# Multi-query attention on one core: in even steps a norm's small operation, a query product and the lower scores' addition change places with the upper reciprocals

## The chip, the cores and the metric

The kernel runs on 1 core of one Trainium2 chip. The metric is the device time of one execution in microseconds (us); less is better. A core has five engines, each with a queue of its own that it works off in order: TensorE (PE, with its weight loads shown as PEld), VectorE (DVE), ScalarE (ACT), GpSimd (POOL) and SyncE (SP), which here only issues DMAs.

## The reference

There are 64 sequences of 128 tokens with 512 features, all float32. The attention has 16 query heads of width 64 and one shared key and value head:

```python
xn = layernorm(x, g_in)
q = (xn @ Wq) * 64 ** -0.5            # 16 heads of 64
k, v = split(xn @ Wkv)                # one head of 64, and a null key and value in front
sim = q @ k.T + attn_bias             # causal, and masked by a mask per sequence
out = softmax(sim) @ v                # 16 heads of 64 -> 1024
out = layernorm(out @ Wo, g_out)
return x + out
```

## The kernel before, in words

A block is one sequence. Four blocks form a group, since the query projection of a group is worked out together. `step(n)` is called for n = -6 to 62; it holds, in an order written out by hand, pieces of work on many blocks: it multiplies attention weights and values of block n (`values`, `values_end`), takes the softmax of block eb = n + 1 and the scores of block nb = n + 2, projects a quarter of a later group's queries and finishes the output of earlier blocks. Every call puts its instructions at once at the end of the queues of the engines, so the order of calls in `step` is the order on each engine. Semaphore waits between engines are put in by the framework where a tile is read, written or used again. A pool's tile waits until all readers of the tile that had its buffer are done.

What the change and the prediction's steps touch:

- **Scores.** `scores(nb, hf)` is made of 32 small matmuls on PE into the one PSUM tile `ps` (lines L500); hf 0 is the lower half of the rows, whose causal keys are 64 of 128, hf 1 the upper half. `scores_add(nb, hf)` (DVE, L513) adds them to the bias and mask that POOL put in S (`bias_add`, L479). As there is one `ps` buffer, `scores(nb, 1)` waits for `scores_add(nb, 0)`. `scores_max` (DVE, L518) gives the maxima.
- **Softmax.** `exps(eb, hf, lo, hi)` is one exponential with a sum for each of the 8 rows of heads (ACT, L527). `rinv(eb, hf)` is the reciprocal of the sums (DVE, L544), `scale` multiplies by it (POOL, L548). `blocks_T` then transposes both halves together (DVE, L580) and `blocks_move` issues the DMAs (SP, L606) that put the pieces in `aTb` for `values` of the next step (PE, L641). `values` of split steps has a small DVE copy named `done` (L673).
- **Queries.** `product(qg, f, k, ...)` is one of seven products of a Strassen-like scheme (4 matmuls of 128x256, PE, L436); they go into the PSUM tiles a and c (one buffer each) and w (two buffers, shared with other tiles). `keep` copies one aside (ACT, L447), `q_out` writes a piece of the queries from PSUM (ACT, L454) or as a sum with a kept piece (DVE, L457). Product 3 of step n + 1 adds into tile c, after `q_out(qg, HC + f, hi_t, "c", "u3")` at the end of step n has read it.
- **Output.** Blocks p and p + 1 (p odd) are projected as a pair in seven products too (`out_product`, 8 matmuls, PE, L755; `out_keep`, L769 on ACT; `out_part`, L776 on ACT or L778 on DVE). `pair_stats` (DVE, L784 to L788), `pair_pow` (POOL, L792), `pair_nmr` (DVE, L799: one operation on 128x1), `pair_norm` (ACT, L809, `yn`) and `pair_residual` (DVE, L813 and L814) make norm and residual; p4 and p4 + 1 are the pair that is finished in a step.
- **Input norm.** `norm_stats` (DVE, L256 to L260; POOL, L261) and `norm_apply` (DVE, L273, `nmr`; ACT, L274) for block m, whose x was loaded by SP in an earlier step. SP also carries the loads of residuals (`res`), the tokens (`xd`, `xT`) and the stores.

In the even steps from 4 to 56, `first` and `third` hold (a pair's first products begin, another pair is finished), and `second` does not. The kernel before gives there, among others, this order:

```python
        if soft and n != 1:
            exps(eb, 1, 2, 4)
        if soft and not second:
            exps(eb, 1, 4, 6)
        if fast:
            product(qg, f, 1, ps_q, "a")
            keep("a", "p1")
            q_out(qg, f, lo_t, "w", "p1")
        if soft and not second:
            exps(eb, 1, 6)
            rinv(eb, 1)
            scale(eb, 1)
```

Of the kernel before, what the change touches and what calls it, by code (L numbers as in the profile page):

```python
# [17 lines left out]
def kernel(  # L18
# [87 lines left out]
    ps_q = ctx.enter_context(tc.tile_pool(name="ps_q", bufs=1, space=PSUM))  # L106
# [147 lines left out]
    def norm_stats(m):  # L254
        st = small.tile([P, 6], FP, tag="st", name=f"st_{m}")
        nc.vector.bn_stats(st, xs[m])  # L256
        mv = small.tile([P, 2], FP, tag="mv", name=f"mv_{m}")
        nc.vector.bn_aggr(mv, st)
        rstd = small.tile([P, 1], FP, tag="rstd", name=f"rstd_{m}")
        nc.vector.tensor_scalar(rstd, mv[:, 1:2], EPS, None, ALU.add)  # L260
        nc.gpsimd.tensor_tensor(rstd, rstd, nhalf, ALU.pow)  # L261
        stats[m] = mv, rstd
# [157 lines left out]
    def product(g, f, k, pool, tag, start=True):  # L420

        if start:
            prod[tag] = pool.tile([P, HT], FP, tag=tag, name=f"p{tag}_{g}_{f}_{k}")
        lo, hi = xT[g][:, 0 : GB // 2], xT[g][:, GB // 2 :]
        t1, t2, t3, t4 = (xS.get((g, i)) for i in range(1, 5))
        w, t = {
            1: (a11, lo[:, :, lo_k]),
            2: (a12, lo[:, :, hi_k]),
            3: (s4, hi[:, :, hi_k]),
            4: (a22, t4),  # L430
            5: (s1, t1),
            6: (s2, t2),
            7: (s3, t3),
        }[k]
        for kc in range(HK):
            nc.tensor.matmul(  # L436
                prod[tag],
                w[:, kc, f * P : (f + 1) * P],
                t[:, :, kc, :],
                start=(start and kc == 0),  # L440
                stop=(kc == HK - 1),
                skip_group_check=not start,
            )

    def keep(tag, name):
        kept[name] = bp.tile([P, HT], FP, tag=f"k{name}", name=f"k{name}", bufs=1)
        nc.scalar.copy(kept[name], prod[tag])  # L447

    def q_out(g, c, toks, tag, name=None):
        lo = toks.start // N  # L450
        o = q_part(g, c, lo, lo + 2)
        p = prod[tag].rearrange("p (t h i) -> p t h i", t=2, h=2)
        if name is None:
            nc.scalar.copy(o, p)  # L454
        else:
            k = kept.pop(name).rearrange("p (t h i) -> p t h i", t=2, h=2)
            nc.vector.tensor_tensor(o, p, k, ALU.add)  # L457
# [57 lines left out]
    def scores_max(b, hf):  # L515
        if hf == 0:
            nmax[b] = small.tile([P, 2, R8], FP, tag="nmax", name=f"nmax_{b}")
        nc.vector.tensor_reduce(  # L518
            nmax[b][:, hf], S[b][:, :, WITH_NULL[hf]], AX.X, ALU.max, negate=True
        )  # L520

    def exps(b, hf, lo=0, hi=R8):
        if hf == 0 and lo == 0:
            rsum[b] = small.tile([P, 2, R8], FP, tag="rsum", name=f"rsum_{b}")
        for k in range(lo, hi):
            row = S[b][:, k, WITH_NULL[hf]]
            nc.scalar.activation(  # L527
                row,
                row,
                AF.Exp,  # L530
                bias=nmax[b][:, hf, k : k + 1],
                accum_out=rsum[b][:, hf, k : k + 1],
            )
# [8 lines left out]
    def rinv(b, hf):  # L542
        rinvs[b, hf] = small.tile([P, R8], FP, tag="rinv", name=f"rinv_{b}_{hf}")
        nc.vector.reciprocal(rinvs[b, hf], rsum[b][:, hf])  # L544
# [178 lines left out]
    def plain(b):  # L723
        return not (paired(b) or paired(b - 1))
# [39 lines left out]
    def out_keep(tag, name, slot):  # L764
        kept[name] = bp.tile([P, HE], FP, tag=f"k{slot}", name=f"k{name}", bufs=1)
        if name == "yu2":
            nc.vector.tensor_copy(kept[name], prod["y" + tag])  # L767
        else:
            nc.scalar.copy(kept[name], prod["y" + tag])  # L769

    def out_part(b, e, tag, name=None):
        if b not in ys:
            ys[b] = hp.tile([P, DIM], FP, tag="y", name=f"y_{b}", bufs=3)
        o = ys[b][:, lo_e if e == 0 else hi_e]
        if name is None:
            nc.scalar.copy(o, prod["y" + tag])  # L776
        else:
            nc.vector.tensor_tensor(o, prod["y" + tag], kept.pop(name), ALU.add)  # L778
# [17 lines left out]
    def pair_nmr(b):  # L796
        mv, rstd = yn.pop(b)
        nmr = small.tile([P, 1], FP, tag="nmro", name=f"nmro_{b}")
        nc.vector.tensor_scalar(nmr, mv[:, 0:1], rstd, -1.0, ALU.mult, ALU.mult)  # L799
        nmrs[b] = nmr, rstd  # L800
# [61 lines left out]
    def step(n):  # L862
        def ok(b, end=B):
            return 0 <= b < end
# [11 lines left out]
        p12, p4, p5673 = n - 1, n - 3, n - 2  # L876
        first, third, second = paired(p12), paired(p4), paired(p5673)
        one = ok(n - 1) and plain(n - 1)
        def transfers():

            if n == 1:
                store(0)
            if n > B3 + 1 and ok(n - 2) and plain(n - 2):
                store(n - 2)
            loads_late(n)
# [22 lines left out]
                token_sum(qg, k)  # L908
        for m in mns:
            norm_stats(m)  # L910
        if n == -4:
            bias_add(0)
            bias_add(1)
# [42 lines left out]
        if n == B3 - 1:  # L956
            scores(B3 + 1, 1)
            scores_add(B3 + 1, 1)
            scores_max(B3 + 1, 1)
        if third:  # L960
            pair_stats(p4 + 1)
        if 2 * GB <= mb < B:
            tokens_T(mb)
            if (mb + 1) % GB == 0:
                tokens_out(mb // GB)
        if soft and n != 1:
            exps(eb, 0, 4)
        if fast and f == 0 and not fill:
            token_sum(qg, 1)
        if soft and n not in (1, B3 + 1):  # L970
            rinv(eb, 0)
            scale(eb, 0)
        if third:
            pair_pow(p4 + 1)
# [29 lines left out]
        if n == B3:  # L1004
            out_keep("X", "yp1", "p1")
            scores(eb, 0)
            scores_add(eb, 0)
            scores_max(eb, 0)
            out_product(p12, 2, ps_w, "w")
            pair_norm(p4)  # L1010
            pair_residual(p4)
            store(p4)
            out_part(p12, 0, "w", "yp1")
            scores(eb, 1)
            scores_add(eb, 1)
            exps_half(eb, 0)
            scores_max(eb, 1)
        elif first:
            out_keep("X", "yp1", "p1")
            out_product(p12, 2, ps_w, "w")  # L1020
            out_part(p12, 0, "w", "yp1")
        if soft and n != 1:
            exps(eb, 1, 2, 4)
        if soft and not second:
            exps(eb, 1, 4, 6)
        if fast:
            product(qg, f, 1, ps_q, "a")
            keep("a", "p1")
            q_out(qg, f, lo_t, "w", "p1")
# [20 lines left out]
        if fast and f == 0 and not fill:  # L1050
            for k in range(3, 5):
                token_sum(qg, k)
        if fast:
            product(qg, f, 5, ps_q, "c")
        if second:
            out_product(p5673, 7, ps_y, "X", start=False)
# [9 lines left out]
        if n == B3 - 1:  # L1066
            exps_half(B3 + 1, 0)
            exps(B3 + 1, 1, 0, 3)
        if sc and n != B3:
            scores(nb, 0)  # L1070
            scores_add(nb, 0)
        split = sc and n != B3
# [207 lines left out]
```

## Time and profile before

| | us |
|---|---|
| median of three runs | 1109.07 |
| the three runs | 1108.53, 1110.0, 1109.07 |
| the profiled execution | 1106.42 |
| its span, first to last instruction | 1104.5 |

| engine | busy us | share of the span |
|---|---|---|
| PE (matmuls) | 1081.3 | 98% |
| PEld (weight loads, beside the matmuls) | 868.1 | 79% |
| DVE | 795.7 | 72% |
| POOL | 706.0 | 64% |
| ACT | 665.5 | 60% |

The profile is of one execution. A row of a timeline has the start in us from the span's begin, the duration in us, engine, line, operation, the tiles out<-in, their shapes, and the count of instructions that were merged; in brackets stand the engine's idle time before it and what ended it. A row of the waits has the waiting engine and tile, what was waited for, the sum in us, the count and the longest. Busy times of different engines overlap; the idle time of an engine that is not the bound costs nothing.

### The profile page before, as it was taken

The page shows a single profiled execution, that of the slowest core. Times are in us where ns is not written, and L with a number is a line of the kernel's source. Part 1 is how long each engine was busy: PE and PEld are TensorE (multiplying, and loading weights), DVE is VectorE, ACT ScalarE, POOL GpSimd, SP SyncE. Part 2 cuts the span into 40 slices and gives each one's busy share as a digit, 9 for nine tenths or more (in the row PEclk, how much of TensorE's full clock was granted, in tenths as well). Part 3 has the DMA queues.
Part 4 walks back from the last instruction along what each step waited for, and adds up shares of the span by engine and source line. Part 5 has one row for each costly group of instructions (what it writes and reads, how often), then busy time and mean ns, then how long its engine had stood idle before and what let it go on. Part 6 is the DMA issues. An engine that isn't in the chain of part 4 may idle for free.

```text
span 1104.5 us, 27326 instructions
## 1 busy us (share of the span) xinstructions
PE 1081.3 (98%) x9794; PEld 868.1 (79%) x9794; DVE 795.7 (72%) x1729; ACT 665.5 (60%) x2645; POOL 706.0 (64%) x521
## 2 busy tenths in 40 slices
PE   8999999999999999999999999999999999999987
PEld 5576788888888888888888888888888888888643
DVE  4676677877867877776886777787777787666852
ACT  3265567666666656566756566766666665657651
POOL 2546958566676756767575675856667675676832
PEclk9999999999999999999999999999999999999999
DMA  6422354453534444353353435445353453422333
GB/s 198 129 76 62 81 150 112 134 131 89 159 99 139 125 128 122 91 167 107 121 138 113 126 101 149 115 131 132 87 159 99 134 130 116 113 63 76 97 106 100
DMA packets 101062, 129.81 MB, mean 118 GB/s; under 512 B 21312, under 2 KB 65728, under 8 KB 99136
## 3 DMA queue, kind: packets, MB, share of 16 engines
q1 hardware_dynamic: 99680, 126.70, 41.0%
q8 instruction: 78, 1.28, 0.5%
q10 hardware_dynamic: 1248, 1.38, 0.4%
q14 instruction: 56, 0.46, 0.1%
HBM read 54.86 MB, written 31.46 MB: 78 GB/s over the span
## 4 chain that ended last, share of the span: by engine, by line
PE 81%; DVE 5%; DMA 4%; ACT 4%; SPq 3%; POOL 2%; issue 1%; DVEq 0%; POOLq 0%; ACTq 0%
PE pa L436 17%; PE pyX L755 16%; PE pc L436 8%; PE pyY L755 8%; PE ps L500 8%; PE po L641 7%; PE pk L321 4%; PE pw L436 4%; PE pyw L755 4%; DMA x<-in_x_dram 3%; PE py L702 3%; ACT s L527 2%; SPq L606 2%; PE pq L387 1%; DVE s L513 1%
## 5 line engine op out<-in xcount | busy, mean ns | idle before, releaser
L527 ACT ACTIVATE s<-s,nmax 128x65 f32<-128x65 f32 (+1 forms) x1024 | 371.5, 367 | 0.0
L479 POOL TENSOR_TENSOR s<-biasp,mneg 128x1552 f32<-128x1552 f32 x64 | 205.3, 3208 | 112.0 <-DVE sb L580 108.8
L548 POOL TENSOR_TENSOR s<-s,rinv 128x512 f32<-128x512 f32 (+1 forms) x128 | 189.6, 1482 | 122.6 <-DVE nmro L799 89.1
L685 ACT ACTIVATE oT<-po,nv 128x512 f32<-128x512 f32 x128 | 81.0, 683 | 198.0 <-PE po L641 198.0
L527 ACT ACTIVATION_READ_ACCUMULATOR s<-s,nmax 128x1 f32 x1024 | 194.7, 190 | 0.0
L755 PE MATMUL pyX<-wT,oT 128*128 128x256 f32 x696 | 164.7, 379 | 0.5 <-DVE kyu L767 0.5
L755 PEld LDWEIGHTS pyX<-wT,oT 128*128 128x128 f32 x696 | 131.8, 190 | 19.6 <-DVE kyu L767 0.9
L500 PEld LDWEIGHTS ps<-kT,qT 64*64 64x64 f32 x4096 | 92.5, 134 | 48.1 <-DVE s L513 25.6
L513 DVE TENSOR_TENSOR s<-ps,s 128x512 f32<-128x512 f32 (+1 forms) x128 | 121.6, 950 | 10.1 <-PE ps L500 9.6
L436 PE MATMUL pa<-xS,wq 128*128 128x256 f32 x480 | 123.6, 380 | 1.0 <-ACT ku L447 1.0
L518 DVE TENSOR_REDUCE nmax<-s 128x8 f32<-128x520 f32 (+1 forms) x128 | 120.1, 938 | 1.3
L500 PE MATMUL ps<-kT,qT 64*64 64x64 f32 (+1 forms) x4096 | 116.7, 251 | 3.7 <-DVE done L673 2.0
L580 DVE STREAM_TRANSPOSE sb<-s 128x1536 f32<-128x1536 f32 x62 | 109.9, 1773 | 11.6 <-POOL s L548 4.3
L641 PE MATMUL po<-aTb,vs 64*64 64x256 f32 (+1 forms) x1240 | 115.3, 379 | 0.0
L436 PEld LDWEIGHTS pa<-xS,wq 128*128 128x128 f32 x480 | 86.2, 190 | 11.2 <-ACT ku L447 1.8
L447 ACT COPY ku<-pa 128x256 f32<-128x256 f32 x120 | 44.7, 373 | 82.5 <-PE pa L436 82.5
L261 POOL TENSOR_TENSOR rstd<-rstd,nhalf 128x1 f32<-128x1 f32 x64 | 35.7, 558 | 60.4 <-DVE rstd L260 55.4
L436 PE MATMUL pa<-xS,wS 128*128 128x256 f32 x240 | 67.8, 405 | 0.1
L809 ACT ACTIVATE yn<-y,nmro,rstdo 128x512 f32<-128x512 f32 x58 | 45.4, 782 | 36.2 <-DVE nmro L799 36.1
L321 PE MATMUL pk<-wkv,xT 128*128 128x128 f32 x488 | 64.5, 275 | 0.0
L457 DVE TENSOR_TENSOR qT<-pw,kp 128x256 f32<-128x256 f32 x60 | 25.4, 424 | 53.4 <-ACT kp L447 53.4
L641 PEld LDWEIGHTS po<-aTb,vs 64*64 64x64 f32 (+1 forms) x1240 | 55.8, 134 | 9.7 <-issue 4.1
(116 smaller groups left out, 2068.9 us busy)
## 6 DMA issues: line engine op xcount, KB each, us to landing
aTb<-sb SPq DMA_DIRECT2D x369, 64.0 KB
x<-in_x_dram SPq DMA_DIRECT2D x64, 256.0 KB
res<-in_x_dram SPq DMA_DIRECT2D x64, 256.0 KB
out_dram<-y SPq DMA_DIRECT2D x64, 256.0 KB
aTb<-sb SPq DMA_DIRECT2D x492, 32.0 KB
xd<-xb SPq DMA_DIRECT2D x14, 1024.0 KB
xT<-xd SPq DMA_DIRECT2D x56, 256.0 KB
wo<-in_L_cond_Wo_dram SPq DMA_DIRECT2D x1, 2048.0 KB
```

The costliest lines, as they stand in the source:

```text
L321: nc.tensor.matmul(pkv, xT[g][:, t, kc, :], wkv[:, kc, :], start=(kc == 0), stop=(kc == KC - 1),)
L436: nc.tensor.matmul(prod[tag], w[:, kc, f * P : (f + 1) * P], t[:, :, kc, :], start=(start and kc == 0), stop=(kc == HK - 1), skip_group_ch ...
L479: nc.gpsimd.tensor_tensor(S[b], biasp, mneg[:, t].unsqueeze(1).broadcast_to([P, R8, ROW]), ALU.add,)
L500: nc.tensor.matmul(pv[u * DH : (u + 1) * DH, r, f, :], qT[g][rows, f, t, hf, u], kT[b][rows, 0:nk], start=True, stop=True,)
L513: nc.vector.tensor_tensor(sv, pss.pop((b, hf)), sv, ALU.add)
L518: nc.vector.tensor_reduce(nmax[b][:, hf], S[b][:, :, WITH_NULL[hf]], AX.X, ALU.max, negate=True)
L527: nc.scalar.activation(row, row, AF.Exp, bias=nmax[b][:, hf, k : k + 1], accum_out=rsum[b][:, hf, k : k + 1],)
L548: nc.gpsimd.tensor_tensor(sv, sv, rinvs.pop((b, hf)).unsqueeze(2).broadcast_to([P, R8, sv.shape[2]]), ALU.mult,)
L580: nc.vector.transpose(sb.rearrange("p j e q -> p e j q"), S[b][:, :, 1 : ROW - 1].rearrange("p e (j k) -> p e j k", k=Q),)
L641: nc.tensor.matmul(pos[b][u][r * DH : (r + 1) * DH, half], vals[keys], aT_of(b)[keys, slots, r * NF : (r + 1) * NF], start=start, stop=Tru ...
L685: nc.scalar.activation(oT[b][:, u * NF : (u + 1) * NF, :].rearrange("p f (s q) -> p s f q", q=Q), po[u].rearrange("p h i f q -> p (h i) f q"),
L755: nc.tensor.matmul(prod[key], h[:, c, :], w[:, c, :], start=(start and c == 0), stop=(c == HC - 1), skip_group_check=not start,)
```

## The change

In the even steps that start one pair, finish another and project queries (`even`; n = 4, 6, ... 56, 27 steps), calls move:

- `pair_nmr(p4)` comes forward to just behind the input norm's statistics.
- The exponentials of the lower half, rows 4 to 8, keep their place on ACT; the lower reciprocal comes ahead of `pair_stats(p4 + 1)` and the token transpose on DVE.
- Query product 1, its copy and its `q_out` come ahead of the out product 2 and its `out_part`; the exponentials between them are dealt out anew around these copies.
- Product 5, the lower scores and their addition come ahead of the last two exponentials, the upper reciprocal, `pair_norm(p4 + 1)` and `norm_apply`. On PE product 5 and the lower scores keep their places; on DVE the addition now stands in front of the upper reciprocal, the `nmro` of block p4 + 1 and the `nmr` of the input norm.
- The kept piece `yp1` uses the slot u3 in place of p1, since p1 is now in use at the same time.

The order on POOL and on SP stays as it was.

```diff
+        even = first and third and fast
+
...
         for m in mns:
             norm_stats(m)
+        if even:
+            pair_nmr(p4)
...
+        if even:
+            exps(eb, 0, 4)
+            rinv(eb, 0)
         if third:
             pair_stats(p4 + 1)
...
-        if soft and n != 1:
+        if soft and n != 1 and not even:
             exps(eb, 0, 4)
         if fast and f == 0 and not fill:
             token_sum(qg, 1)
         if soft and n not in (1, B3 + 1):
-            rinv(eb, 0)
+            if not even:
+                rinv(eb, 0)
             scale(eb, 0)
...
+        elif even:
+            out_keep("X", "yp1", "u3")
+            product(qg, f, 1, ps_q, "a")
+            exps(eb, 1, 2, 4)
+            keep("a", "p1")
+            q_out(qg, f, lo_t, "w", "p1")
+            out_product(p12, 2, ps_w, "w")
+            out_part(p12, 0, "w", "yp1")
+            exps(eb, 1, 4, 6)
+            product(qg, f, 5, ps_q, "c")
+            scores(nb, 0)
+            scores_add(nb, 0)
         elif first:
             out_keep("X", "yp1", "p1")
             out_product(p12, 2, ps_w, "w")
             out_part(p12, 0, "w", "yp1")
-        if soft and n != 1:
+        if soft and n != 1 and not even:
             exps(eb, 1, 2, 4)
-        if soft and not second:
+        if soft and not second and not even:
             exps(eb, 1, 4, 6)
-        if fast:
+        if fast and not even:
             product(qg, f, 1, ps_q, "a")
...
-        if fast:
+        if fast and not even:
             product(qg, f, 5, ps_q, "c")
...
-        if sc and n != B3:
+        if sc and n != B3 and not even:
             scores(nb, 0)
             scores_add(nb, 0)
```

## The prediction

> **What bounds the kernel now.** I read the page's engine table first, then the list of waits, then the timelines of single steps.
>
> ```profile
> PE 1081.3 (98%) x9794; PEld 868.1 (79%) x9794; DVE 795.7 (72%) x1729; ACT 665.5 (60%) x2645; POOL 706.0 (64%) x521
> PEclk9999999999999999999999999999999999999999
> ```
>
> TensorE (PE) is busy 98% of the span at full clock. So a change of order can only win what is left of PE's stalls, and any new wait in front of PE is paid in full. The list of waits says where PE's weight loads sit:
>
> ```profile
> PEld ps L500 <- DVE s L513: 25.6, 61, 1.7
> ...
> DVE st L256 <- DMA x<-in_x_dram: 5.4, 11, 1.1
> ```
>
> The first row is the wait of the upper scores (`scores(nb, 1)`) for the lower scores' addition (`scores_add(nb, 0)`), which frees their PSUM buffer. 25.6 us is not all to be won: I took from PE's timeline, for each of the 27 steps that the change touches (even n, 4 to 56), the time from the first lower score matmul to the first upper one. It is 1.51 us in every step of the kind n = 4, 8, 12 ... (and in most odd steps), because even an addition that starts at once needs 0.76 us until the lower scores are out, 0.69 us itself and 0.06 us for the signal. In the steps n = 6, 10, 14 ... it is 1.57, 1.65, 1.64, 1.73, 1.89, 2.37, 1.51, 2.20, 2.54, 1.68, 2.18, 1.51, 1.51. The excess over 1.51 sums to 4.4 us; this is all that the addition's new place can win. Step 26 shows how it arises (PE, then DVE):
>
> ```profile
> 504.91 0.69 PE L500 MATMUL ps<-kT,qT 64*64 64x64 f32 x32
> 507.28 1.10 PE L500 MATMUL ps<-kT,qT 64*64 64x128 f32 x32 [0.23 <-DVE done L673]
> ```
>
> ```profile
> 499.13 0.69 DVE L256 BATCH_NORM_STATS2 st<-x 128x6 f32<-128x512 f32 x1 [0.60 <-DMA x<-in_x_dram]
> ...
> 505.44 0.42 DVE L457 TENSOR_TENSOR qT<-pw,kp 128x256 f32<-128x256 f32 x1 [0.49 <-ACT kp L447]
> 506.22 0.20 DVE L544 RECIPROCAL rinv<-rsum 128x8 f32<-128x8 f32 x1 [0.35 <-ACT s L527]
> ...
> 506.54 0.68 DVE L513 TENSOR_TENSOR s<-ps,s 128x512 f32<-128x512 f32 x1
> ```
>
> A late load of x makes DVE late; the first `nmro` follows behind it, ScalarE (ACT) waits 1.80 us for that before its `yn`, its last exponentials end late, the upper reciprocal (L544) waits for them, and the addition (L513) queues behind the reciprocal. The scores ended before 505.7, the addition began at 506.54.
>
> The step n = 28 is one of the clean ones:
>
> ```profile
> 538.91 0.16 DVE L799 TENSOR_SCALAR nmro<-mvo,rstdo 128x1 f32<-128x1 f32 x1
> ...
> 539.13 0.69 DVE L513 TENSOR_TENSOR s<-ps,s 128x512 f32<-128x512 f32 x1
> ...
> 540.22 0.69 DVE L813 TENSOR_TENSOR yn<-yn,gob 128x512 f32<-128x512 f32 x1
> 540.95 0.69 DVE L814 TENSOR_TENSOR y<-yn,res 128x512 f32<-128x512 f32 x1
> 541.56 1.77 DVE L580 STREAM_TRANSPOSE sb<-s 128x1536 f32<-128x1536 f32 x1
> ...
> 544.95 0.41 DVE L457 TENSOR_TENSOR qT<-pc,ku 128x256 f32<-128x256 f32 x1
> ```
>
> ```profile
> 545.70 0.84 PEld L436 LDWEIGHTS pc<-xT,wS 128*128 128x128 f32 x4
> ```
>
> The last DVE row empties PSUM tile c for `product 3` of the next step, whose first weights load at 545.70. It ends at 545.36: it is 0.34 us ahead. In the other even steps the lead is 0.34 to 0.48 us.
>
> **The change, part by part.** Every instruction stays; only places move.
>
> *Small operation of the first norm (`pair_nmr(p4)`) and exponentials' reciprocal forward.* On ACT nothing but `yn` moves nearer: it no longer waits for DVE's `nmro` (0.68 us in step 28, 1.80 in step 26). Working ACT's rows on from the end of its exponentials (yn every 0.72, keep 0.27, an exponential 0.39), its last exponential of step 28 ends at 537.8 instead of 538.8. ACT is not on PE's path there, so this alone is worth nothing; it is what makes the reciprocal ready.
>
> *Product 1 before the out product.* 0.86 us of PE work changes places with 1.73. Its buffer a was emptied by ACT (498.48 in step 26), 2.9 us before its new place: no wait. The copy yp1 moves to the slot u3, whose reader ended in the step before. DVE's two adds swap, both done before the scores (538.0 against 539.13 in step 28): zero. If x is as late as in the worst step (38) and 0.65 us more (see below), the hops from its statistics to the addition, added up from the rows of step 26, end 0.3 us after the lower scores' start; the addition can't start before 0.76. So the excess goes in all steps: **-4.4 us**.
>
> *Upper reciprocal, second `nmro` and nmr behind the addition.* This is the new wait, in all 27 steps, the clean ones too. In step 28 `nmro` stood ahead of the addition at 538.91; now: addition 539.13, reciprocal 0.61 later (as `done` follows it in step 26), `nmro` +0.12 (506.22 to 506.34), ACT's `yn` +0.20, DVE's L813 +0.81, L814 +0.73, the transpose +0.61. That is 542.21 instead of 541.56: the transpose is **0.65 us later**. The scaling on POOL (reciprocal +0.28, lasting 1.91) ends at 541.93 and is not later than that. Behind the transpose DVE is in order without a pause: L518 +1.69, L513 +0.57, L457 +1.13, ending at 546.01 instead of 545.36. Its signal takes 0.05 us, as in an early stall of the same pair (L457 ends 104.75, load at 104.80), and there the next group's load follows 0.76 us later, not 0.86 as in the flow. So the group behind product 3 starts at 546.82, where it started at 546.56: **0.26 us of PE stall**, in 26 steps (4 to 54): **+6.8 us**. Step 56 is followed by other work: there the next scores load at 1003.63 behind an addition that ends at 1003.49; 0.65 later is +0.57 us.
>
> What else hangs on the later transpose: its 14 DMAs on SP start 0.65 later, with the loads of res and x behind them. The moved blocks landed 1.3 to 2.7 us before the first value product after an even step: covered (it would cost 0.65 less 0.26 a step without). x comes up to 0.65 later in steps 6, 10 ..., covered as counted above. The next step's DVE catches up at its wait for `kp` (1.1 us of idle): nothing more.
>
> ACT's second `yn` starts at 1.69 us after the lower scores, its nmr product 0.72 later, then oT about 0.74 behind: 3.15, where it started at 3.11 released by PE. The key transpose behind oT was reached with 0.72 (step 0) to 0.83 us; that leaves 0.1: zero, with an end of 0.32 a step, below.
>
> The Trainium skill, "VectorE: DVE Perf Modes", section "The DRAIN you can't avoid", says that the next op does not start until the pipe is empty. The rows disagree here: `done` starts at 507.14, with L513 of step 26 running to 507.22, and `nmro` before the reciprocal's end. By the rule reciprocal and `nmro` would each come 0.08 us later than reckoned, 4.2 us more in 26 steps; I take the rows.
>
> Sum: -4.4 + 6.8 + 0.6 = **+3.0 us**. The profiled execution took 1106.42 (span 1104.5, 1.92 around it), so 1109.4 in its like. The median of the three runs is 2.65 above that; with the same distance, **1112.1 us**.
>
> **Rivals.** *Product 3 stays covered (faster).* The stall exists only if DVE comes more than 0.40 us later (lead 0.34 plus the 0.10 by which a stalled group is quicker, less the signal); I reckon 0.65. Should the second `yn` or the transpose come 0.25 us sooner than its hops say, the win is left alone: -4.4, 1104.7. For it: the lead was up to 0.48 behind late steps. Against: every hop is from a row, and the lead is 0.36 or less in all clean steps. Between lies a half: stalls of 0.1 give 1107.9.
>
> *The late loads weigh more in the timed runs (no change).* If the 2.65 us between median and profiled execution are waits for x, the win is 7.0 and the sum +0.4: 1109.5. For: these are what differed from step to step. Against: no row of the timed runs shows it.
>
> *ACT too holds PE (slower still).* If `yn`, nmr and oT do not overlap and the reciprocal and `nmro` follow without overlap, oT comes 0.32 late, the transpose 0.81, and product 3 waits 0.42: 26 x 0.42 + 0.6 - 4.4 = +7.1, 1116.2.
>
> **How the numbers follow.** Stalled product 3 as reckoned 0.50; covered, wholly or mostly, 0.22; balanced by late loads 0.18; ACT too 0.10. 0.2% is 2.2 us, about what a measurement of this kernel can tell from no change. The reckoned case lies just beyond it and loses a little to "same", the covered case is faster but for its half: faster 0.21, same 0.22, slower 0.57. The range takes in most of the covered case below and most of the ACT case above: 1105.4 to 1115.6; the likeliest case alone is 1110.5 to 1114.
>
> **What would show it.** Right: in the clean even steps the time from lower to upper scores stays 1.51, in the others it falls to 1.51; the transpose starts at about 3.84 us after the lower scores (3.19 before); a new row of PE loads of c waiting for DVE's L457, 26 times and some 0.3 us; oT at 3.1 to 3.2. Wrong: no such row (covered), or loads of pk waiting for oT (ACT), or excess left in steps 26, 34, 38, 46 (late x still counts).

## The result, and the profile after

The changed kernel took 1114.99 us (median of five runs, 1112.45 to 1116.21) beside 1108.53 us (five runs, 1107.4 to 1110.0) of the kernel before: a ratio of 1.0056, 95% interval 1.0039 to 1.0073, so it is slower by 6.2 us (4.3 to 8.1). The profiled execution of the changed kernel took 1114.99 us with a span of 1113.1; against the one before (1106.42 and 1104.5) that is 8.6 us more. The two profiles are thus 2.1 us further apart than the medians, because the profiled execution of before lies below its five timed runs. The engine table of the page after:

```profile
PE 1086.7 (98%) x9794; PEld 867.6 (78%) x9794; DVE 799.3 (72%) x1729; ACT 659.9 (59%) x2645; POOL 705.5 (63%) x521
PEclk9999999999999999999999999999999999999999
```

The instructions and the clock are those of before. PE's busy time is no guide here: it rose by 5.4 us with the same 9794 matmuls. The rows of product 3 in step 28 show how. Before, they begin at 545.91, 0.17 us ahead of the end of the rows in front (545.05, lasting 1.03); after, at 549.43, 0.05 us behind it (548.35, lasting 1.03). A stall first eats up the overlap of two groups of rows, and little of it shows as idle time. The list of waits tells more (us in total, times, longest). Before:

```profile
PEld pc L436 <- DVE qT L457: 1.9, 2, 1.1
...
PEld pk L356 <- ACT oT L685: 1.6, 4, 1.0
...
PE po L641 <- DMA aTb<-sb: 1.3, 1, 1.3
```

After:

```profile
PEld ps L500 <- DVE s L513: 24.2, 51, 2.4
...
DVE st L256 <- DMA x<-in_x_dram: 14.0, 14, 2.2
...
PEld pc L436 <- DVE qT L457: 9.1, 19, 1.1
...
PEld pk L356 <- ACT oT L685: 3.6, 15, 1.0
...
PE po L641 <- DMA aTb<-sb: 2.6, 6, 0.9
```

The upper scores' wait for the addition fell by only 1.4 us (25.6 before). VectorE's wait for x went from 5.4 to 14.0. The row of `pc` is the new wait of product 3 for tile c: 17 waits more than before, where both stood in the kernel's start, and not 26 as forecast. The key transpose waits for oT a little more often (`pk`), and value products for moved blocks longer (`po`).

Step 28, whose rows of before the prediction shows, looks like this after (DVE, then PE's weight loads, then ACT). Its lower scores start at 541.68; before, they started at 538.37.

```profile
542.44 0.69 DVE L513 TENSOR_TENSOR s<-ps,s 128x512 f32<-128x512 f32 x1 [1.09 <-PE ps L500]
543.05 0.19 DVE L544 RECIPROCAL rinv<-rsum 128x8 f32<-128x8 f32 x1
543.16 0.16 DVE L799 TENSOR_SCALAR nmro<-mvo,rstdo 128x1 f32<-128x1 f32 x1
...
545.58 1.77 DVE L580 STREAM_TRANSPOSE sb<-s 128x1536 f32<-128x1536 f32 x1
...
548.97 0.41 DVE L457 TENSOR_TENSOR qT<-pc,ku 128x256 f32<-128x256 f32 x1
```

```profile
549.43 0.73 PEld L436 LDWEIGHTS pc<-xT,wS 128*128 128x128 f32 x4 [0.46 <-DVE qT L457]
550.19 0.84 PEld L755 LDWEIGHTS pyY<-wT,yS 128*128 128x128 f32 x4
```

```profile
543.42 0.78 ACT L809 ACTIVATE yn<-y,nmro,rstdo 128x512 f32<-128x512 f32 x1 [2.30 <-DVE nmro L799]
...
544.85 1.24 ACT L685 ACTIVATE oT<-po,nv 128x512 f32<-128x512 f32 x2
```

The reader is to see that the addition, reciprocal, `nmro`, `yn`, transpose and L457 follow each other as the prediction worked them out, and that product 3's weights now stand behind L457 (549.38, load at 549.43). The transpose starts 3.90 us after the lower scores (3.19 before), the group behind product 3 8.51 after them (8.19 before): 0.32 us of stall. The 13 steps n = 4, 8, ... all have this wait; their length, from lower scores to the next lower scores, went from 17.13 to 17.45 us.

In the steps n = 6, 10, ... (the late steps, below) the addition now also starts 0.76 us after the scores, as it was meant to, but upper scores still come late in some. Step 30 (its lower scores start at 574.60), PE, then DVE:

```profile
574.60 0.69 PE L500 MATMUL ps<-kT,qT 64*64 64x64 f32 x32
575.11 0.60 PE L641 MATMUL po<-aTb,vs 64*64 64x256 f32 x4
576.63 0.43 PE L641 MATMUL po<-aTb,nv 64*64 64x256 f32 x2 [0.92 <-DMA aTb<-sb]
...
577.13 0.39 PE L500 MATMUL ps<-kT,qT 64*64 64x128 f32 x4
```

```profile
569.99 0.69 DVE L256 BATCH_NORM_STATS2 st<-x 128x6 f32<-128x512 f32 x1 [2.19 <-DMA x<-in_x_dram]
...
575.36 0.69 DVE L513 TENSOR_TENSOR s<-ps,s 128x512 f32<-128x512 f32 x1 [0.15 <-PE ps L500]
```

The addition is done at 576.05; the upper scores come at 577.13. What they stand behind on PE are value products that wait for a block moved by DMA.

In the late steps product 3 waits less often. Its weights can load 7.75 us after the lower scores, when L457 has emptied tile c. In steps 6, 14, 18, 50 and 54 PE arrives there sooner and waits 0.14 to 0.46 us. In the other eight PE is late itself, through late blocks, and there is no wait; those steps are 17.55 to 18.50 us long. So within one step the two delays do not add up: the longer one counts, and 17.45 us is a floor that product 3 puts under all 26 steps.

**The ledger.** The 8.6 us between the two profiles are: the floor of product 3, 26 x 0.32 = +8.3; the excess of steps 6, 10, ... beyond the clean length (17.13 before, the floor of 17.45 after), 4.7 before and 3.6 after, -1.1; steps 5, 9, ..., 15.40 before and 15.47 after in twelve of them, 12 x 0.07 = +0.8; step 56 from lower scores to the next, 6.77 before and 7.42 after, +0.65; the part ahead of step 4 +0.55; the rest -0.6. Without the floor: the 13 steps 4, 8, ... are 4.2 us longer, and the 13 late steps together exceed 17.13 by 7.8 us instead of 4.7.

### The profile page after: what moved, and what is told of

Same layout as the page of the kernel before. It is cut to its first block, busy times and chain, and to the rows that moved or that the text cites. A ratio compares the mean times of both kernels' runs of the same rounds, so it can differ in the third digit from the quotient of the medians.

```text
span 1113.1 us, 27299 instructions
## 1 busy us (share of the span) xinstructions
PE 1086.7 (98%) x9794; PEld 867.6 (78%) x9794; DVE 799.3 (72%) x1729; ACT 659.9 (59%) x2645; POOL 705.5 (63%) x521
## 4 chain that ended last, share of the span: by engine, by line
PE 74%; DMA 9%; DVE 7%; SPq 6%; ACT 2%; issue 1%; POOL 1%; DVEq 0%; ACTq 0%; POOLq 0%
PE pyX L755 15%; PE pa L436 14%; PE pyY L755 8%; PE pc L436 8%; PE ps L500 6%; PE po L641 6%; DMA x<-in_x_dram 5%; SPq L606 5%; PE pyw L755 4%; PE pk L321 3%; PE pw L436 3%; PE py L702 3%; DMA out_dram<-y 3%; DVE sb L580 2%; DVE s L513 2%; PE pq L387 2%
## 5 line engine op out<-in xcount | busy, mean ns | idle before, releaser
L500 PEld LDWEIGHTS ps<-kT,qT 64*64 64x64 f32 x4096 | 96.6, 134 | 46.3 <-DVE s L513 24.2
L500 PE MATMUL ps<-kT,qT 64*64 64x64 f32 (+1 forms) x4096 | 120.1, 250 | 4.9 <-DVE s L513 2.5
L641 PE MATMUL po<-aTb,vs 64*64 64x256 f32 (+1 forms) x1240 | 121.2, 380 | 0.0
L641 PEld LDWEIGHTS po<-aTb,vs 64*64 64x64 f32 (+1 forms) x1240 | 58.4, 134 | 9.8 <-issue 4.1
L436 PE MATMUL pc<-xT,wS 128*128 128x256 f32 x240 | 63.4, 387 | 1.5 <-DVE qT L457 0.8
```

What stands on the lines that cost most here:

```text
L436: nc.tensor.matmul(prod[tag], w[:, kc, f * P : (f + 1) * P], t[:, :, kc, :], start=(start and kc == 0), stop=(kc == HK - 1), skip_group_ch ...
L500: nc.tensor.matmul(pv[u * DH : (u + 1) * DH, r, f, :], qT[g][rows, f, t, hf, u], kT[b][rows, 0:nk], start=True, stop=True,)
L641: nc.tensor.matmul(pos[b][u][r * DH : (r + 1) * DH, half], vals[keys], aT_of(b)[keys, slots, r * NF : (r + 1) * NF], start=start, stop=Tru ...
```

## The experiments

My first theory was that the addition's new place alone makes the changed kernel slower: it delays reciprocal, `nmro` and so the transpose, which makes product 3 wait, and it also makes the DMAs behind the transpose late, so that the gain in steps 6, 10, ... is lost again. The rivals were that other moved parts cost the time, that the late blocks come from the late steps' own transposes, and, at the end, that DMA transport and not the order on SP makes blocks late.

The table gathers what the traces gave. "Excess" is the sum over the 13 steps 6, 10, ... 54 of their length beyond the clean length: 17.13, or the floor that product 3 sets where the transpose is late in them (17.45; 17.39 in add_only, 17.15 in nmr_ahead). In brackets stands the same sum beyond 17.13. Lateness of less than 0.32 us vanishes under the higher floor, so only kernels with the same floor can be compared by it. Further, "x" VectorE's waits for x in steps 4 to 56; "SP" SP's waits for a load of x in front of a block move (L606), from the list of SP's own waits; "T" the transpose's start after the lower scores in steps 4, 8, ...; "5, 9" the sum of the 13 steps 5, 9, ...; all in us.

| kernel | step 4, 8 ... | T | excess | x | SP | 5, 9 ... | ratio to before, 95% |
|---|---|---|---|---|---|---|---|
| before | 17.13 | 3.16 | 4.7 | 4.7 | 9.6 | 200.2 | 1 |
| changed | 17.45 | 3.89 | 3.6 (7.8) | 12.6 | 16.8 | 201.0 | 1.0056 (1.0039 to 1.0073) |
| add_back | 17.13 | 3.16 | 3.0 | 5.0 | 8.0 | 200.3 | 0.9964 (0.9950 to 0.9978) |
| add_only | 17.39 | 3.83 | 8.4 (11.8) | 14.2 | 16.7 | 201.0 | 1.0064 (1.0046 to 1.0082) |
| nmr_only | 17.13 | 3.16 | 2.9 | 5.8 | 8.8 | 200.2 | 0.9978 (0.9964 to 0.9992) |
| nmr_ahead | 17.15 | 3.58 | 7.7 (8.0) | 12.3 | 15.9 | 201.0 | 1.0000 (0.9989 to 1.0012) |
| q_first | 17.13 | 3.89 | 2.6 | 9.2 | 19.1 | 210.4 | 1.0070 (1.0053 to 1.0088) |
| q_first_act | 17.13 | 3.89 | 6.9 | 11.3 | 14.1 | 201.1 | 1.0011 (0.9999 to 1.0022) |
| ahead_4k | 17.45 | 3.89 | 4.9 | 9.8 | 14.9 | 201.0 | 1.0033 (1.0020 to 1.0045) |
| ahead_4k2 | 17.13 | 3.16 | 0.9 (5.1) | 5.4 | 9.4 | 200.3 | 0.9987 (0.9974 to 1.0000) |
| loads_first | 17.44 | 3.89 | 0.3 (4.5) | 0 | 23.4 | 215.1 | 1.0143 (1.0122 to 1.0165) |
| back_loads | 17.13 | 3.16 | 1.0 | 0 | 24.8 | 216.7 | 1.0102 (1.0080 to 1.0125) |
| x_act | 17.45 | 3.89 | 0.4 (4.6) | 0 | 0.9 | 201.4 | 1.0042 (1.0026 to 1.0058) |
| back_x_act | 17.13 | 3.16 | 0.2 | 0 | 5.3 | 201.9 | 0.9957 (0.9941 to 0.9973) |

**add_back: the changed kernel with the addition at its old place**

```diff
         elif even:
...
             product(qg, f, 5, ps_q, "c")
-            scores(nb, 0)
-            scores_add(nb, 0)
...
-        if sc and n != B3 and not even:
+        if sc and n != B3:
             scores(nb, 0)
             scores_add(nb, 0)
```

> The changed kernel with the lower scores' addition put back behind the upper reciprocal, the second nmro and the nmr; all that came forward (first nmro, lower reciprocal, product 1) stays forward. Theory 1, the late transpose: the reciprocal and nmro behind the addition make the transpose 0.7 us late in every even step, and both prices come from that: product 3 waits 0.3 us (8 us in 26 steps), and SP's loads behind the block moves come later, so that the moved blocks are late in steps 6, 10, 14 ... Then here the transpose is at 3.2 us after the lower scores, no product 3 waits, the excess over 1.51 us from lower to upper scores falls from 4.4 us to 1 or less: 1104 to 1105 us, 0.3 to 0.4% faster than before. Theory 2, the blocks are late anyway: the late addition of before only hid them; then product 3's wait goes but an excess of about 4 us stays: 1108 to 1109, like before. Theory 3, what came forward costs by itself: slower than before, 1110 or more.

Measured: 1105.0 us (1102.48 to 1106.8) beside 1109.54, faster than both kernels. The waits of this kernel:

```profile
PEld ps L500 <- DVE s L513: 23.8, 56, 2.9
...
DVE st L256 <- DMA x<-in_x_dram: 5.1, 8, 1.7
```

Product 3's wait is back to the 1.9 us of the start, and x's wait is what it was before. The time is what the first theory said, the excess is not: 3.0, where it said 1 or less and the second theory about 4. So some lateness of the late steps is there with the old place of the addition too. The rest of the change wins 0.36%, and the addition's place costs 0.92% (1.0056 less 0.9964), 10.2 us. The profiles say where: spans 1113.1 and 1102.8, 10.3 apart, of which 8.3 are the floor of product 3, 0.7 are steps 5, 9, ..., 0.65 is step 56 and 0.6 the excess.

**add_only: the kernel before with product 5 and the addition ahead of the last exponentials, nothing else**

```diff
+        if even:
+            product(qg, f, 5, ps_q, "c")
+            scores(nb, 0)
+            scores_add(nb, 0)
         if soft and not second:
             exps(eb, 1, 6)
             rinv(eb, 1)
             scale(eb, 1)
```

> The kernel before with one thing of the change alone: product 5, the lower scores and their addition stand ahead of the last two exponentials' reciprocal, the second nmro and the nmr. Nothing else comes forward. Theory 1: this alone is the price: transpose 0.7 us late, product 3 waits 0.3 us in 26 steps, 1113 to 1116 us like the changed kernel. Theory 3: the price lies in what came forward, so this is near before, 1107 to 1110.

Measured: 1116.33 us (1114.07 to 1119.11) beside 1109.54. The move alone does all the harm, and without the early `nmro` the excess is even 8.4.

**nmr_only: the kernel before with the first `nmro` forward alone**

```diff
         for m in mns:
             norm_stats(m)
+        if first and third and fast:
+            pair_nmr(p4)
```

> The kernel before with one move: the first nmro of an even step comes forward behind the input norm's statistics. The order of product 1, reciprocals and addition is as before. If the chain late x, nmro, ACT's yn, last exponentials, upper reciprocal, addition is what holds the addition in steps 6, 10 ..., ACT's 0.7 to 2.0 us wait for nmro falls and most of the excess of 4.4 us goes: 1105 to 1107 us. If product 1's or the lower reciprocal's new place is needed for that: 1108 to 1109, like before.

Measured: 1105.09 us (1103.56 to 1109.28) beside 1108.16. This one operation of 128x1, which ACT's first `yn` waited for, brings the same fall of the excess as add_back, to 2.9 against 3.0. By the times it is 0.22% of add_back's 0.36%, with intervals that overlap.

**nmr_ahead: the changed kernel with the second `nmro` ahead of the addition**

```diff
             product(qg, f, 5, ps_q, "c")
+            pair_nmr(p4 + 1)
             scores(nb, 0)
             scores_add(nb, 0)
```

> The changed kernel with the second nmro put ahead of the addition; the upper reciprocal and the nmr of the input norm stay behind it. Theory 1 with ACT's yn as the link that sets the transpose (nmro, yn, residual, transpose): yn can start before the scores are out, and the transpose waits for POOL's scaling, at 3.6 us after the lower scores in place of 3.9; product 3 waits 0.1 us or less: 1107 to 1110 us. Were the reciprocal and POOL's scaling the link that sets it: transpose still at 3.9, 1114 to 1116.

Measured: 1109.42 us (1108.14 to 1112.14) beside 1109.54. Waits:

```profile
DVE st L256 <- DMA x<-in_x_dram: 12.9, 12, 2.5
PEld pc L436 <- DVE qT L457: 4.1, 16, 1.1
```

The transpose starts at 3.58 instead of 3.89, and that 0.31 us is what product 3 wins: the step is 17.15 long. So product 3 begins to wait when the transpose is about 0.4 us later than before (3.58 less 3.16, with 0.02 of stall), which is the bound of 0.40 that the prediction named. The excess and x's waits stay high: they do not hang on product 3.

**q_first: the changed kernel with the last `q_out` ahead of the upper scores' addition in even steps**, so that tile c is read sooner

```diff
             scores(nb, 1)
-            scores_add(nb, 1)
+            if not even:
+                scores_add(nb, 1)
...
+            if even:
+                scores_add(nb, 1)
```

> The changed kernel with one more move in the even steps: the upper scores' addition (1.13 us on DVE) stands behind the query piece that empties tile c, in front of the maxima. The transpose stays 0.7 us late. Theory 1: tile c is emptied 1.1 us sooner, product 3 does not wait: 8 us less, 1106 to 1108 us; the excess of about 4 us in steps 6, 10 ... stays, since SP's loads are still late. Should the wait for tile c be only a sign of something else that is late by as much, 1112 to 1115.

Measured: 1116.68 us (1115.08 to 1118.31) beside 1109.54: a miss. The wait of product 3 is gone (17.13 with the transpose still at 3.89), but twelve of the steps 5, 9, ... became 16.25 long. Step 29, DVE and PE's weight loads:

```profile
557.18 2.31 DVE L465 TENSOR_SCALAR mneg<-m 128x256 f32<-128x256 uint8 x2 [0.25 <-POOL s L479]
559.41 0.41 DVE L778 TENSOR_TENSOR y<-pyY,kyu 128x256 f32<-128x256 f32 x1
559.75 0.68 DVE L513 TENSOR_TENSOR s<-ps,s 128x512 f32<-128x512 f32 x1
```

```profile
558.12 0.56 PEld L500 LDWEIGHTS ps<-kT,qT 64*64 64x64 f32 x32 [0.33 <-issue]
...
560.48 0.86 PEld L500 LDWEIGHTS ps<-kT,qT 64*64 64x64 f32 x32 [1.25 <-DVE s L513]
```

The addition begins 1.6 us after its scores, because VectorE first converts the mask (L465, two operations), which here lasts 2.31 us. Why it lasts so long is told in the last section; the expectation knew nothing of it.

**q_first_act: q_first with the mask converted by ACT in steps 5, 9, ...** (lines of the trace are shifted by up to nine)

```diff
+    def mask_act(g):
+        m8 = m8s.pop(g).rearrange("p (t j) -> p t j", t=GB)
+        for keys, m in ((LK, m8[:, :, 0:NL]), (UK, m8)):
+            nc.scalar.activation(
+                mneg[:, :, keys], m, AF.Identity, bias=negc, scale=-NEG
+            )
...
-                mask_neg(qg)
+                mask_act(qg)
```

> q_first with the mask of steps 5, 9, 13 ... made by two ScalarE operations in place of the two on VectorE (the value is the same). In q_first no product 3 waited, but in these steps the addition of the lower scores stood behind the mask operation, which ended 0.15 us after POOL's scaling whatever its own length (1.1 us before, 1.5 with the change, 1.9 in q_first). If the mask operation is held by POOL's scaling, it no longer stands in DVE's queue here, the steps 5, 9 ... fall from 16.25 to 15.40 us: 10 to 11 us less than q_first, 1105 to 1107. If the upper maxima, which came later in q_first, hold these steps, they stay: 1114 to 1117.

Measured: 1109.0 us (1107.1 to 1114.04) beside 1108.16. Steps 5, 9, ... are 15.47 again, so the mask was what q_first paid for there. That they are not 15.40 has a cause of its own: in the trace the addition waits for POOL as well as for PE here, with a separate wait instruction (0.02 us) in front of it, and starts 0.83 us after its scores instead of 0.76, with VectorE idle. The time is still 2 us above the top of what was expected, and the waits say why:

```profile
DVE st L258 <- DMA x<-in_x_dram: 11.9, 12, 2.0
...
PE po L650 <- DMA aTb<-sb: 2.8, 5, 0.9
```

With product 3 free and the mask out of the way the excess is 6.9, counted from 17.13. The transposes are at 3.89 here as in the changed kernel. A late transpose thus costs something in steps 6, 10, ... that has nothing to do with product 3. Beyond 17.45 these steps exceed by 3.5 us here and by 3.6 in the changed kernel: the lateness is the same, and the floor of product 3 hid half of it. That q_first has an excess of only 2.6 fits its longer steps 5, 9, ..., which give the moves 0.85 us more; this is argued, not tested.

**ahead_4k and ahead_4k2: the addition forward only in steps 4, 8, ..., or only in steps 6, 10, ...** (`n % 4 == 0`, for the second `n % 4 == 2`)

```diff
-            scores(nb, 0)
-            scores_add(nb, 0)
+            if n % 4 == 0:
+                scores(nb, 0)
+                scores_add(nb, 0)
...
-        if sc and n != B3 and not even:
+        if sc and n != B3 and not (even and n % 4 == 0):
```

> The changed kernel with the addition ahead of the upper reciprocal only in the steps 4, 8, 12 ... 56; in steps 6, 10, 14 ... it is back behind reciprocal, nmro and nmr, as in add_back (1105.0 us). Theory 1: the late transpose of steps 4, 8 ... moves SP's loads of x and the block moves behind them, and this is what makes x and the moved blocks late in the steps 6, 10 ...: 13 product 3 waits of 0.32 (4.2 us) and an excess of 3 us or more in steps 6, 10 ...: 1111 to 1114. Theory 2 (the lateness has its cause in the late steps themselves): the excess stays at 1 us or less: 1108 to 1110.

> The other half: the addition is ahead of the upper reciprocal only in the steps 6, 10, 14 ... 54, and behind it in 4, 8, 12 ... Theory 1: 13 product 3 waits (4.2 us), but x and the blocks come in time, the excess is 1 us or less, as in add_back: 1109 to 1110. Theory 2: the excess of 3 us or more is here: 1111 to 1114.

Measured beside 1108.16: ahead_4k 1111.5 us (1110.8 to 1113.9), ahead_4k2 1106.89 (1104.93 to 1109.29). Where the addition is forward only in steps 6, 10, ..., their excess falls to 0.9, against 3.6 in the changed kernel with the same floor, and x's waits stay at 5.4: most of the gain that the prediction reckoned is there. It is no less lateness than in add_back, whose late steps also exceed 17.45 by 0.9 us. Where it is forward only in steps 4, 8, ..., x's waits double to 9.8 and the excess of the steps 6, 10, ..., in which nothing is changed against add_back, is 4.9 against add_back's 3.0. So lateness travels from a step 4, 8, ... to the step 6, 10, ... two steps on. The time of ahead_4k2 lies below both expectations, by 2 us and more. Product 3 waits ten times more than before in it, not the 13 times that were expected:

```profile
PEld pc L436 <- DVE qT L457: 5.7, 12, 1.1
```

**loads_first and back_loads: SP's loads of res and x ahead of the block moves in steps 4, 8, ...**, on the changed kernel and on add_back

```diff
+        soon = even and n % 4 == 0
+        if soon:
+            transfers()
...
-        if n < B3:
+        if n < B3 and not soon:
             transfers()
```

> The changed kernel, but in the steps 4, 8, 12 ... SP issues the loads of res and x in front of the 14 block moves and the four xT loads, not behind them. The transpose stays 0.7 us late, product 3 still waits 0.32 us in 26 steps. If the blocks and x are late in steps 6, 10 ... because the late transpose pushes these two loads into the time of the next step's block moves, x comes some 10 us sooner, VectorE's waits for x fall from 12.6 us to 3 or less, PE's idle time at the value products of these steps from 6.6 to about 2.5: 1110 to 1113. If the moves themselves are what is late, the two loads (1.2 us of SP) in front make it worse: 1116 to 1119.

> The same order of SP's loads in add_back (1105.0 us), where the transpose is in time and no product 3 waits. What is left there in steps 6, 10 ... is 3.0 us. If late x and the collision of its load make it, 1 us or less stays: 1102 to 1104. If the moves that are now 1.2 us later in steps 4, 8 ... hold the value products of steps 5, 9 ...: 1106 or more.

Measured beside 1109.91: loads_first 1126.06 us (1123.09 to 1128.14), back_loads 1121.12 (1118.38 to 1126.92), both far slower, loads_first beyond both of its forecasts. The load of x now goes out 4.2 to 5.9 us after the lower scores of steps 4, 8, ..., ahead of the moves. VectorE's waits for x are gone and so is the excess (0.3 and 1.0). But the moves of the same step are late instead, and steps 5, 9, ... pay with some 15 us. The fourteenth move of steps 4 to 48 is issued 16.2 to 17.7 us after the lower scores; in the changed kernel it is issued at 14.2 to 15.1.

**x_act and back_x_act: the load of x in steps 4, 8, ... issued by ACT**, on the changed kernel and on add_back (lines of the trace are shifted by one)

```diff
-    def load_x(m):
+    def load_x(m, queue=nc.sync):
...
-            nc.sync.dma_start(
+            queue.dma_start(
                 out=xs[m], in_=x[g * GB : (g + 1) * GB, t * Q : (t + 1) * Q, :]
...
-                load_x(m)
+                early = 4 <= n < B3 and n % 4 == 0
+                load_x(m, nc.scalar if early else nc.sync)
```

> The changed kernel; in steps 4, 8, ... the load of x is issued by ACT instead of SP, at ACT's pause of 1.40 us behind the copy ku of the step's end; nothing else moves. Theory Q (the order on SP's queue): in the changed kernel each DMA on SP waits for the one issued eight places before it; the 10 us load of x, issued 18.3 us after the lower scores of step 28, so holds back moves of step 29 (14 waits of SP for x, 16.8 us), and their blocks come late for the values of step 30. With the load on ACT, SP's waits for x go (under 3 us), VectorE's waits for x fall from 14.0 to under 3, and the late steps' excess falls from 3.6 to about 1 us, with the 26 waits of product 3 of 0.32 us left: 2.6 us less than the changed kernel, ratio to the kernel before about 1.0033, 1111 to 1114 us, and steps 5, 9, ... stay at 15.47. Theory T (transport): an early load of x slows the moves in the DMA engines themselves, wherever it is issued; then steps 5, 9, ... become 0.5 us or more longer, as when the loads stood first on SP, and the time is 1118 us or more.

> The changed kernel with the addition of the lower scores at its old place, and in steps 4, 8, ... the load of x issued by ACT instead of SP. Theory Q (the order on SP's queue): what is left there of late x and late blocks in steps 6, 10, ... (3.0 us of excess) falls to about 1, no wait of product 3: 2 us less than the 1105.0 us without the load's move, so 1102 to 1104, ratio to the kernel before about 0.9945. Theory T (transport): the early load slows the moves of steps 4, 8, ..., steps 5, 9, ... become 0.5 us or more longer: 1111 us or more.

What stood behind this pair was SP's own list of waits and SP's timeline around step 29. Before, then after:

```profile
SPq L606 <- DMA x<-in_x_dram: 9.6, 11, 1.5
```

```profile
555.31 0.61 SPq L120 DMA_DIRECT2D x<-in_x_dram  x1
...
559.40 9.77 SPq L606 DMA_DIRECT2D aTb<-sb  x14
```

```profile
SPq L606 <- DMA x<-in_x_dram: 16.8, 14, 2.6
```

```profile
559.98 0.62 SPq L120 DMA_DIRECT2D x<-in_x_dram  x1
...
563.03 12.04 SPq L606 DMA_DIRECT2D aTb<-sb  x14
```

A block move does not read x. It waits because each DMA on SP waits for the DMA issued eight places before it in that queue (the trace's DMA semaphores are eight, used in turn). The eighth behind the load of x is the seventh move of step 29. The load is issued by step 28 behind its late moves, 18.30 us after that step's lower scores against 16.95 before, and lands 10 us later, at 569.96; the sixth move was out by 567.34, the seventh starts at 569.99, and the fourteen take 12.04 us instead of 9.77.

Measured beside 1108.37: x_act 1112.91 us (1111.55 to 1115.65), back_x_act 1103.91 (1100.95 to 1105.87), both in the range of the theory of the queue, though the ratio of back_x_act is short of the 0.9945 expected. Waits of x_act:

```profile
PEld pc L437 <- DVE qT L458: 13.4, 27, 1.1
...
DVE st L257 <- DMA x<-in_x_dram: 1.0, 2, 0.6
...
PE po L642 <- DMA aTb<-sb: 0.6, 2, 0.3
```

```profile
SPq L607 <- DMA x<-in_x_dram: 0.9, 2, 0.5
```

Of the changed kernel's excess 0.4 us is left, and the time from lower to upper scores is 1.51 us in 12 of the 13 steps. With the blocks in time product 3 waits in nearly all of the 26 steps, 25 times more than before, as the prediction said. The load also goes out earlier, 4.15 us after the lower scores of step 28 instead of 18.30. That the queue counts, and not the earlier time alone, is shown by the two kernels with the loads first: there x is loaded about as early, on SP, and the moves behind it are late. A late load on ACT was not run. Steps 5, 9, ... of x_act stay at 15.47 but for two (15.51 and 15.77), although x is now loaded while the moves run. Transport does slow the moves a little: the fourteenth is issued at 15.0 to 15.8 us (14.2 to 15.1 in the changed kernel), now behind landings of earlier moves and stores (SP's waits for those are 8.8 and 6.2 us). In back_x_act three of the steps 5, 9, ... take 15.87 to 16.07 instead of 15.40, 1.6 us in all, which gives back more than half of the excess won there. That is an eighth or less of the 14 to 16 us of the two kernels with the loads first, whose cause is thus mostly the order on SP. Between the changed kernel and x_act lies what the late x and the late blocks cost: ratios 1.0056 and 1.0042, spans 1113.1 and 1111.1. The intervals of the ratios overlap, so the profile's rows carry this, not the times. back_x_act is the fastest version, 0.9957 (0.9941 to 0.9973); it is not told apart from add_back.

## Why the prediction was right or wrong

**Right: direction and main mechanism.** The kernel is slower, inside the range, and by the new wait of product 3 for L457 first of all. Transposes were reckoned at 3.84 and came at 3.89; clean steps keep 1.51 between the two scores; step 56 cost 0.65 against 0.57. oT came at 3.17 against 3.15, and the key transpose behind it at 3.88 instead of 3.85: the row of waits for oT, a sign that was named for the rival "ACT too", grew by 2 us, but these 0.03 us a step lie ahead of product 3's wait, which takes them in. The number alone would have misled: 1114.99 lies above the 1110.5 to 1114 of the likeliest case, nearer to the 1116.2 of "ACT too", which did not come, than to the 1112.1 reckoned. The reciprocal followed the addition by 0.61 and `nmro` the reciprocal by 0.11 in step 28, as the rows' hops had it; the reciprocal started 0.08 us before the addition's row ends. The Trainium skill, page "VectorE: DVE Perf Modes", section "The DRAIN you can't avoid", gives the rule that the prediction quotes, and adds that a next op that is not held starts earlier. The rows are like this second case, so they do not contradict the page, as the prediction took it.

**Mis-sized: product 3.** 0.26 us a step were reckoned; 0.32 came, in all 13 clean steps and as a floor under the other 13: 8.3 for 6.8 us. The forecast of 26 waits failed, since in eight late steps PE was later than the floor. The hop that was short is the one from `nmro` to `yn`, taken as 0.20 and measured as 0.26 (543.16 to 543.42). The threshold of 0.40 was right (nmr_ahead).

**Failed: "So the excess goes in all steps: -4.4 us."** The first half held: the addition starts 0.76 us after the scores in every step. But 3.6 of 4.7 us stayed, -1.1 for -4.4. A sign of being wrong that the prediction had named, excess left in steps 26, 34, 38 and 46, is there: 1.68, 2.10, 1.78 and 2.00 us from lower to upper scores. The cause is not the one named with it: the addition was in time, the blocks were late. The step that failed is the paragraph on what else hangs on the later transpose. It called the moved blocks covered, from their landing before the first values behind an even step, and x covered, from its hops to the addition. Each was true of its own step: by the landings in the trace the last move of an even step came 0.5 to 2.4 us before those values in the kernel before (closer than the 1.3 to 2.7 of the prediction) and 0.1 to 2.2 us before them in the changed one. What it left out is that SP's queue goes on: the load of x stands behind the late moves, and the moves of the next, odd step stand behind that load and wait for it, so blocks come late for the values two steps on. Some of this was there before and hidden behind the late addition: add_back, with the addition as before and the first `nmro` early, keeps 3.0 us. The late transpose made it more. ahead_4k2 shows most of the 4.4 (excess 0.9, so -3.8) where no late transpose precedes; ahead_4k shows that the added lateness comes from steps 4, 8, ...; x_act, beside loads_first, shows that it goes by SP's queue.

**Not foreseen: +0.8 us in steps 5, 9, ...** POOL's upper scaling in step 29 starts 1.80 us before the lower scores of that step (557.33 and 559.13), where it started 2.20 before (553.30 and 555.50); the mask is converted beside it and ends later by as much (last section), and the addition behind it on VectorE starts 0.85 instead of 0.76 us after its scores. POOL is late because VectorE is. Before, then after:

```profile
548.11 0.55 POOL L261 TENSOR_TENSOR rstd<-rstd,nhalf 128x1 f32<-128x1 f32 x1
549.14 1.05 POOL L548 TENSOR_TENSOR s<-s,rinv 128x512 f32<-128x512 f32 x1 [0.48 <-DVE rinv L544]
```

```profile
552.13 0.55 POOL L261 TENSOR_TENSOR rstd<-rstd,nhalf 128x1 f32<-128x1 f32 x1 [0.64 <-DVE rstd L260]
553.16 1.05 POOL L548 TENSOR_TENSOR s<-s,rinv 128x512 f32<-128x512 f32 x1 [0.49 <-DVE rinv L544]
```

The late transpose puts the rows behind it on VectorE 0.7 us later against the lower scores of step 28 (L260 at 9.51 before and 10.21 after), POOL now waits for them, and 0.32 of the 0.7 is the step's own growth. The other kernels with this mask conversion and their loads in the old order agree: 200.2 or 200.3 where the transposes of steps 4, 8, ... are early (add_back, nmr_only, ahead_4k2), 201.0 where they are late (add_only, ahead_4k).

The rival "product 3 stays covered" failed on its condition, a transpose 0.25 us sooner than reckoned; "late loads weigh more" had the opposite sign: x's waits rose from 5.4 to 14.0.

By size the forecast of +3.0 stood for a measured +6.2 (4.3 to 8.1); in the profile's own terms +3.0 for +8.6, and the two terms above, 1.5 and 3.3, with the 0.8, are its 5.6.

## What to carry to other kernels

When an operation moves up an in-order queue, list everything it passes, and follow each to the next reader of a single buffer one step on: here 0.7 us on a reciprocal and a 128x1 operation put a floor 0.32 us higher under 26 steps of TensorE. Follow DMAs through their own queue for more than one step, and look at the issuing engine's list of waits for moves that wait for a load they don't read: the place of a long load in a queue matters as much as its own due time, and another engine's queue may carry it for less. Where two delays end at the same place, the longer one counts: a wait that is seen in 17 of 26 steps can still be the floor under all of them, and taking it away uncovers the other. Of a change with several parts, run the cheap parts alone: one 128x1 operation brought as much of the excess as all that came forward.

## What the runs showed of the hardware that I had not expected

**VectorE's mask conversion waits for GpSimd.** L465 writes float32 from uint8, two operations. Step 29 after and then before, each with POOL's scaling beside it:

```profile
557.85 1.87 DVE L465 TENSOR_SCALAR mneg<-m 128x256 f32<-128x256 uint8 x2
```

```profile
557.33 1.90 POOL L548 TENSOR_TENSOR s<-s,rinv 128x1024 f32<-128x1024 f32 x1
```

```profile
554.22 1.48 DVE L465 TENSOR_SCALAR mneg<-m 128x256 f32<-128x256 uint8 x2
```

```profile
553.30 1.91 POOL L548 TENSOR_TENSOR s<-s,rinv 128x1024 f32<-128x1024 f32 x1
```

The pair ends 0.49 us after the scaling's end in both, 0.48 in q_first, however early it starts: 1.48, 1.87 and 2.31 us long. In the trace the first, smaller operation is the one that is held (1.14, 1.53 and 1.98 us; 0.24 to 0.28 in the few places without POOL beside it), the second takes its 0.41. The Trainium skill, page "SBUF — State Buffer", section "Who interferes with whom", says that a `tensor_scalar` may take a port pair that VectorE shares with GpSimd, and that whichever comes second is blocked for the whole instruction. The rows agree; that it is this port they can't show. ACT converts the same mask in 0.51 to 0.71 us an operation (q_first_act), with POOL's scaling beside it in step 29.

**DMA queue.** A DMA on SP waits for the one eight places before it to land (SP's waits for x, 8.0 to 24.8 us in the kernels that load it on SP alone). With 0.65 us an issue eight places are some 5 us by estimate. The loads of x in steps 4 to 48 took 8.8 to 10.2 us to land in the changed kernel and 8.3 to 9.6 before, so a load in the midst of moves holds them back. Where that time goes stays open.
